# Transposing gathered rows on two row halves, ahead of the products, in a graph network's edge loop

## The chip, the cores and the metric

The kernel runs on one core of one Trainium2 chip. The metric is device time in microseconds (us) of one execution, as the median of several runs. The engines have these names in the profile: PE is TensorE (PEld its weight loads), DVE VectorE, ACT ScalarE, POOL GpSimd, SP SyncE.

## What is computed

One message-passing layer of a graph network on 6250 nodes with 128 features and 100000 edges, with a residual and a layer norm. All data are float32. The edges come sorted by destination.

```python
row, col = src, dst                                   # 100000 each
msg_in = concat([x[row], x[col]], axis=-1)            # 256 features
h = relu(msg_in @ Wm1 + bm1)                          # 256
h = relu(h @ Wm2 + bm2)                               # 256
messages = h @ Wm3 + bm3                              # 128
agg = segment_sum(messages, col) / clip(count(col), 1)
upd = relu(concat([x, agg]) @ Wn1 + bn1) @ Wn2 + bn2
out = layernorm(x + (x + upd))
```

## The kernel before

**Preparation.** `x[row] @ Wm1[:128]` equals a row of `A = x @ Wm1[:128]`, so the kernel computes A (`atab`) and B = x @ Wm1[128:] (`btab`, as three bfloat16 terms) once a node and keeps both in DRAM. It also turns the edge lists into columns: `srcT[:, g, j]` holds, for tile j of edge group g, the source row number of the edge that stands on each of the 128 partitions. `src_f` is the float copy of the list from which these columns are transposed (`columns`).

**The edge loop.** A group is 512 edges, four tiles of 128; there are 196 groups. The loop works on two groups at a time, 98 pairs, and is written out in Python as a pipeline of several stages with the order of TensorE, ScalarE, GpSimd, VectorE and SyncE written out by hand. One turn holds, on TensorE and in this order, work of four different pairs:

- `turned` (L594): six transposes of the partial sums of an older pair, which `add_up` (L603) on VectorE adds to the accumulator `acc`, eight windows of nodes.
- `first_layer` (L544, L549): the 128 x 256 tiles of gathered A rows are transposed into PSUM (`ph`, four banks: two groups i, two halves h of a group's columns), eight transposes of 128 x 128 a group; onto the same PSUM columns come the products of `bw` (rows of B for a narrow window of destinations, bfloat16) with `ohts`, a 0/1 matrix that spreads them over the edges, four a group. ScalarE adds the bias and applies relu (L556) and makes `h1`.
- `sums` (L575): a 0/1 matrix `oh` of 32 columns a tile adds up h2 over the edges of each node of a window. The four tiles of a group use four column groups of the array.
- `second_layer` (L565): h1 times `w2`, in four parts of two tiles each; VectorE applies bias and relu behind each part (L567) and makes `h2s[0]`, `h2s[1]`.

A float32 product of L565 or L575 stands in the profile as two matmul records, a transpose as one.

**The gathers.** `fetch` (L506) issues eight indirect DMAs a pair from GpSimd, one for each tile, with the row numbers in a column of `srcT`; they fill `rows`, which has two buffers. A pair's rows are thus fetched while the pair before it is still to be transposed: the first gather of a pair waits until the products of the pair two before it have read the buffer. Ahead of five of the eight gathers GpSimd copies one column (`seen`, L505) of something that ScalarE or VectorE has made; `made_by` says which:

```python
return {2: h1[:, 1, 1, 0:1], 3: h1[:, 0, 0, 0:1], 4: h2s[0][:, 0, 0:1], 5: h2s[0][:, 2, 0:1],
        7: h2s[1][:, 0, 0:1]}
```

That copy holds the queue of GpSimd until the named part of h1 or h2 is there. The SyncE queue brings the rows of B (L511), the ScalarE queue the edges' offsets `db` (L390).

After the loop, products over the nodes, the second half of the update, the layer norm and the stores make up the rest.

Of the kernel before, what the change touches and what calls it, by code (L numbers as in the profile page):

```python
# [9 lines left out]
F32 = mybir.dt.float32  # L10
BF16 = mybir.dt.bfloat16
I32 = mybir.dt.int32
# [7 lines left out]
P = 128  # L20
# [7 lines left out]
def kernel(  # L28
# [36 lines left out]
    nc = tc.nc  # L65
# [4 lines left out]
    GT = 4  # L70
    GE = GT * P
# [7 lines left out]
    NQ = 2 * WN  # L79
# [13 lines left out]
    srcT = const.tile([P, NG, GT], I32, name="srcT")  # L93
# [17 lines left out]
    ident = const.tile([P, P], F32, name="ident")  # L111
# [40 lines left out]
    with tc.tile_pool(name="prep", bufs=1) as prep, tc.tile_pool(  # L152
        name="brow", bufs=6
    ) as brow, tc.tile_pool(name="pp", bufs=3, space=PSUM) as pp, tc.tile_pool(
        name="pb", bufs=5, space=PSUM
# [4 lines left out]
        src_i = prep.tile([R, 2 * GE], I32, name="src_i", tag="src_i")  # L160
# [59 lines left out]
        nc.vector.tensor_reduce(most, real.rearrange("r s (j e) -> r (s j) e", j=GT), AX.X, ALU.max)  # L220

        src_f = prep.tile([R, 2, GT, P], F32, name="src_f", tag="dst_i")
        nc.vector.tensor_copy(src_f.rearrange("r s u e -> r (s u e)"), src_i)
        span_i = prep.tile([R, RT], I32, name="span_i")

        nc.vector.tensor_tensor(most, most, least, op=ALU.max)
# [217 lines left out]
        behind = list(X_BEHIND)  # L444
# [29 lines left out]
    with edge, tc.tile_pool(name="wk", bufs=2) as wk, tc.tile_pool(  # L474
        name="p1", bufs=1, space=PSUM
# [8 lines left out]
        h2s = [wk.tile([P, GT, H + 1], F32, name=f"h2_{i}", bufs=1) for i in range(NH2)]  # L484
# [6 lines left out]
        def flat_bank():  # L491
            return bank().rearrange("p t h -> p (t h)")

        seen = wk.tile([P, 1], F32, name="seen", bufs=1)

        def fetch(groups, queues, behind={}):


            rows = ld.tile([P, 2, (GT + 1) * H], F32, name="rows", bufs=2)
            got = []  # L500
            for i, ((idx, firsts), queue) in enumerate(zip(groups, queues)):
                ag = rows[:, i, :GT * H].rearrange("p (j h) -> p j h", j=GT)
                for j in range(GT):
                    if i * GT + j in behind:
                        nc.gpsimd.tensor_copy(seen, behind[i * GT + j])  # L505
                    nc.gpsimd.indirect_dma_start(  # L506
                        out=ag[:, j, :], out_offset=None, in_=atab[:, :],
                        in_offset=bass.IndirectOffsetOnAxis(ap=idx[:, j:j + 1], axis=0))
                bw = rows[:, i, GT * H:].bitcast(BF16).rearrange("p (k h) -> p k h", k=2)
                for h, first in enumerate(firsts):  # L510
                    queue.dma_start(bw[:, h, :], btab[ds(first, NW)].rearrange("n c h -> (n c) h")[:P])  # L511
                got.append((ag, bw))
            return got
# [21 lines left out]
            return oht, oh[:, :GT]  # L535


        def first_layer(got, ohts, nts):
            ph = p1.tile([P, 2, 2, HC, 2 * P], F32, name="ph")
            for i, ((ag, bw), nt) in enumerate(zip(got, nts)):  # L540
                for c in range(HC):
                    for j in range(nt):
                        h, k = divmod(j, 2)
                        nc.tensor.matmul(ph[:, i, h, c, k * P:(k + 1) * P], ag[:, j, c * P:(c + 1) * P], ident,  # L544
                                         is_transpose=True, start=(c == 0 and k == 0), stop=False,
                                         skip_group_check=True)
                for c in range(HC):
                    for h in range(nt // 2):
                        nc.tensor.matmul(ph[:, i, h, c, :], bw[:, h, c * P:(c + 1) * P],  # L549
                                         ohts[:, i, h * 2 * P:(h + 1) * 2 * P], start=False, stop=True,  # L550
                                         skip_group_check=True)
            h1 = wk.tile([P, 2, HC, GE], F32, name="h1")
            for i in reversed(range(len(nts))):
                nh = nts[i] // 2
                for c in range(HC):
                    nc.scalar.activation(h1[:, i, c, :nh * 2 * P].rearrange("p (h e) -> p h e", h=nh),  # L556
                                         ph[:, i, :nh, c, :], AF.Relu, bias=b1[:, c:c + 1])
            return h1

        def second_layer(h1, h2, nt):  # L560
            for j0 in range(0, nt, 2):
                ph2 = bank()
                for j in range(j0, j0 + 2):
                    for c in range(HC):
                        nc.tensor.matmul(ph2[:, j - j0, :], h1[:, c, j * P:(j + 1) * P],  # L565
                                         w2[:, c, :], start=(c == 0), stop=(c == HC - 1))
                nc.vector.tensor_tensor(h2[:, j0:j0 + 2, :H], ph2, nb2.to_broadcast([P, 2, H]), op=ALU.max)  # L567

        def sums(groups):

# [61 lines left out]
        NP = NG // 2  # L632
# [11 lines left out]
        def load_firsts(p):  # L644
            st[p]["firsts"] = [load_bases(tilei[0:1, g * GT:(g + 1) * GT], NTS[g], ENG.DVE) for g in (2 * p, 2 * p + 1)]

        def made_by(i):
            if i < 3:
                return {}
            h1 = st[i - 2]["h1"]  # L650
            return {2: h1[:, 1, 1, 0:1], 3: h1[:, 0, 0, 0:1], 4: h2s[0][:, 0, 0:1], 5: h2s[0][:, 2, 0:1],
                    7: h2s[1][:, 0, 0:1]}

        slots = list(range(SLOTS))

        def clear(n):
# [5 lines left out]
        for i in range(NP + 4):  # L662
            if i == 8:
                late_loads()

                none = wk.tile([16, (NG * GE - E) // 16 + 1], I32, name="none", bufs=1)
                nc.vector.memset(none, NONE)
                nc.sync.dma_start(dpad[E - 16:].rearrange("(p e) -> p e", p=16), none)
                nc.sync.dma_start(dpad[:E].rearrange("(p e) -> p e", p=16), dst.rearrange("(p e) -> p e", p=16))
            if i < NP:  # L670
                c = 2 * i // CG + 1
                if 2 * i % CG == 0 and 1 < c < NG // CG:
                    chunks[c] = chunk(c)
                queues = [(nc.sync, ENG.SP), (nc.scalar, ENG.Activation) if i == 0 else (nc.sync, ENG.SP)]
                firsts = [load_bases(pairi[0:1, g * 2:(g + 1) * 2], NTS[g] // 2, eng, NPAD - NW)
                          for g, (_, eng) in zip((2 * i, 2 * i + 1), queues)]
                got = fetch([(srcT[:, 2 * i + k, :], firsts[k]) for k in range(2)], [q for q, _ in queues],
                            made_by(i))
                st[i] = dict(nts=NTS[2 * i:2 * i + 2], got=got)
            p = i - 1  # L680
            if p < 0:
                continue
            if p == 0:
                make_hot(0)
            k = p - 3
            if k >= 0:
                if k < NP - 2:
                    load_firsts(k)
                firsts = st[k]["firsts"]
                pt = turned(st[k]["part"], st[k]["nts"])  # L690
                if k == NP - 1:
                    whole(rest)
                add_up(pt, firsts, st.pop(k)["nts"])
            for step, after in enumerate((10, 12, 13)):
                if i >= after and (i - after) % 4 == 0 and (i - after) // 4 < len(pieces):
                    double((i - after) // 4, step)
            if p + 1 < NP:
                make_hot(p + 1)
            if p == 0:
                clear(3)  # L700
            if p < NP:
                s = st[p]
                s["h1"] = first_layer(s.pop("got"), s.pop("ohts"), s["nts"])
            if p == 0:
                whole(x_part(X_FIRST, bank, (nc.scalar, nc.vector)))
            if 0 <= p - 2 < NP:
                st[p - 2]["part"] = part_of(summed(p - 2), st[p - 2]["nts"])
            if 0 <= p - 1 < NP:
                s = st[p - 1]
                for j, nt in enumerate(s["nts"]):  # L710
                    if p == NP and j == 1:
                        load_firsts(NP - 2)
                        load_firsts(NP - 1)
                    second_layer(s["h1"][:, j], h2s[j], nt)
            if p in (1, 2):
                clear(2)
        assert not st and not slots
# [6 lines left out]
        with tc.If(groups > 0):  # L724
            with tc.For_i(0, NG, 1) as g:
# [3 lines left out]
                with tc.For_i(0, more, 1):  # L729
                    for t, by in ((tilei[0:1, ds(g * GT, GT)], float(WB)), (pbase[:, ds(g, 1), :], float(WB)),  # L730
                                  (dloc[:, ds(g, 1), :], -float(WB))):
                        nc.vector.tensor_scalar(t, t, by, None, op0=ALU.add)
                    idx = wk.tile([P, GT], I32, name="idx")
                    nc.vector.tensor_copy(idx, srcT[:, ds(g, 1), :].rearrange("p o j -> p (o j)"))
                    pbc = wk.tile([P, 2], F32, name="pbc")
                    nc.vector.scalar_tensor_tensor(pbc, pbase[:, ds(g, 1), :].rearrange("p o k -> p (o k)"),
                                                   float(NPAD - NW), iota_p.to_broadcast([P, 2]),
                                                   op0=ALU.min, op1=ALU.add)
                    dl = wk.tile([P, GT], F32, name="dl")
                    nc.vector.tensor_copy(dl, dloc[:, ds(g, 1), :].rearrange("p o j -> p (o j)"))  # L740

                    ti = wk.tile([1, GT], I32, name="ti", bufs=1)
# [242 lines left out]
```

## Time and profile before

| | |
|---|---|
| median of three runs | 1281.67 us (1280.34 to 1282.84) |
| the profiled execution | 1284.33 us |
| its span, first to last instruction | 1282.5 us |
| granted TensorE clock, mean | 0.994 |
| TensorE busy | 1260.3 us, 98% |
| VectorE, ScalarE, GpSimd busy | 649.6, 379.3, 922.6 us |
| gathers (L506) | 784, 981 ns each |
| GpSimd copies (L505) | 475, 199 ns each |
| transposes of gathered rows (L544) | 1564 matmuls, 273 ns each as recorded |

Matmul records overlap, since TensorE is pipelined: the time that one takes of the engine is the step from its start to the next one's start, not its duration. A row of the timeline gives start, length, engine, line, operation, output <- inputs, rows x columns of the array in use, shape, count, and in brackets the idle time before it with what ended that. A row of a group gives total busy time, mean duration in ns, and idle time before the group's instructions.

### The profile page before, as it was taken

What the parts mean: (1) busy time and instruction counts of PE and PEld (TensorE: products, weight loads), DVE (VectorE), ACT (ScalarE), POOL (GpSimd) and SP (SyncE); (2) the same over time, 40 slices, a digit from 0 to 9 for tenths busy, and PEclk for the clock granted to TensorE, in tenths of its full rate; (3) what the DMA queues carried; (4) which work ended last, traced back from release to release, by engine and by line L of the source; (5) the groups of instructions that cost most, each with busy time, mean ns of one, the idle gap of its engine ahead of it and who ended that gap; (6) DMA issues with size and microseconds to landing.
All of it is one profiled execution on the core that took longest, in us unless ns stands there. A gap on an engine that the chain in (4) does not pass through costs nothing. (4 is left out here: it accounts for less than half of the span.)

```text
span 1282.5 us, 25680 instructions
## 1 busy us (share of the span) xinstructions
PE 1260.3 (98%) x8291; PEld 1046.3 (82%) x8292; DVE 649.6 (51%) x1684; ACT 379.3 (30%) x768; POOL 922.6 (72%) x1341
## 2 busy tenths in 40 slices
PE   7999999999999999999999999999999999999998
PEld 5758888888888888888888888888888888888666
DVE  6774444444445444444444444444444444444677
ACT  4652222222222222222222222222222222222156
POOL 5658887777777777777778777777777777785032
PEclk9899999999999999999999999999999999999999
DMA  5976555555555555545555545544455544453153
GB/s 176 356 251 174 153 149 155 143 161 157 140 148 158 151 151 156 150 138 157 159 146 151 143 144 140 144 141 132 139 142 141 144 136 134 138 145 98 34 159 103
DMA packets 147517, 193.52 MB, mean 151 GB/s; under 512 B 23248, under 2 KB 100578, under 8 KB 147364
## 3 DMA queue, kind: packets, MB, share of 16 engines
q0 software_dynamic: 38160, 103.75, 29.9%
q1 hardware_dynamic: 94528, 62.02, 15.6%
q10 hardware_dynamic: 14692, 26.09, 6.8%
q8 instruction: 66, 1.08, 0.3%
q14 instruction: 71, 0.58, 0.1%
HBM read 169.06 MB, written 23.08 MB: 150 GB/s over the span
## 5 line engine op out<-in xcount | busy, mean ns | idle before, releaser
L506 POOL DMA_INDIRECT rows<-atab,srcT x784 | 769.2, 981 | 246.9 <-issue 114.5
L565 PE MATMUL bank<-w,h 128*128 128x256 f32 x3128 | 701.4, 382 | 0.1
L565 PEld LDWEIGHTS bank<-w,h 128*128 128x128 f32 x3128 | 586.1, 190 | 116.3 <-PE bank L575 39.7
L567 DVE TENSOR_TENSOR h<-bank,nb 128x512 f32<-128x512 f32 x391 | 270.8, 693 | 521.1 <-PE bank L565 506.9
L556 ACT ACTIVATE h<-ph,b 128x512 f32<-128x512 f32 x392 | 236.8, 687 | 820.2 <-PE ph L549 820.2
L603 DVE TENSOR_TENSOR acc<-acc,bank 128x63 f32 x782 | 172.6, 221 | 67.5 <-DVE h L567 34.2
L544 PE MATMUL ph<-ident,rows 128*128 128x128 f32 x1564 | 203.8, 273 | 1.4 <-ACT h L556 0.8
L544 PEld LDWEIGHTS ph<-ident,rows 128*128 128x128 f32 x1564 | 177.6, 142 | 3.7 <-ACT h L556 1.7
L549 PE MATMUL ph<-oht,rows 128*128 128x256 bf16 x782 | 118.2, 274 | 1.7 <-DMA rows<-btab 1.7
L575 PE MATMUL bank<-h,oh 128*32 128x257 f32 x1564 | 105.5, 386 | 0.6 <-DVE acc L603 0.6
L505 POOL COPY seen<-h 128x1 f32<-128x1 f32 x475 | 94.7, 199 | 2.0
L549 PEld LDWEIGHTS <-rows 128*128 128x128 bf16 x782 | 76.7, 98 | 8.8 <-DMA rows<-btab 2.0
L594 PE MATMUL bank<-ident,part 128*128 128x128 f32 x588 | 80.3, 272 | 0.0
L594 PEld LDWEIGHTS bank<-ident,part 128*128 128x128 f32 x588 | 69.9, 140 | 10.4 <-issue 0.4
L575 PEld LDWEIGHTS bank<-h,oh 128*32 128x32 f32 x1564 | 40.8, 109 | 38.4 <-DVE acc L603 19.4
L583 ACT COPY part<-bank 128x257 f32<-128x257 f32 x196 | 65.3, 402 | 14.0 <-PE bank L575 14.0
L808 POOL TENSOR_TENSOR agg<-total,rc 128x512 f32<-128x512 f32 (+2 forms) x15 | 16.0, 1070 | 74.3 <-DVE total L805 36.0
L273 PE MATMUL pbt<-w,xT 128*128 128x256 f32 x196 | 47.6, 390 | 10.3 <-DVE rest L298 10.0
L273 PEld LDWEIGHTS pbt<-w,xT 128*128 128x128 f32 x196 | 37.1, 196 | 17.2 <-DVE rest L298 10.7
L518 DVE TENSOR_SCALAR oht<-db,iota_p 128x1024 bf16<-128x1024 bf16 x98 | 47.6, 486 | 0.0
L520 DVE TENSOR_TENSOR oh<-iota_n,dloc 128x256 f32<-128x256 f32 x98 | 40.9, 417 | 0.0
L845 PEld LDWEIGHTS pot<-wu,u 128*128 128x128 f32 x192 | 23.6, 192 | 4.8 <-issue 4.3
(139 smaller groups left out, 446.5 us busy)
## 6 DMA issues: line engine op xcount, KB each, us to landing
db<-reltab ACTq DMA_DIRECT2D x98, 256.0 KB, 4.2
rows<-btab SPq DMA_DIRECT2D x389, 64.0 KB, 3.4
rows<-atab,srcT POOLq DMA_INDIRECT x784
btab<-acc SPq DMA_DIRECT2D x24, 384.0 KB, 5.0
atab<-at SPq DMA_DIRECT2D x24, 256.0 KB, 5.4
xd<-in_x_dram SPq DMA_DIRECT2D x12, 256.0 KB
x2tab<-xd SPq DMA_DIRECT2D x12, 256.0 KB
x_sb<-in_x_dram SPq DMA_DIRECT2D x5, 512.0 KB
```

Of the source, the lines that this page charges most:

```text
L273: nc.tensor.matmul(pbt[:, a, :], xT[:, (t0 + a) * P:(t0 + a + 1) * P], w1[:, k, :], start=True, stop=True)
L505: nc.gpsimd.tensor_copy(seen, behind[i * GT + j])
L506: nc.gpsimd.indirect_dma_start(out=ag[:, j, :], out_offset=None, in_=atab[:, :], in_offset=bass.IndirectOffsetOnAxis(ap=idx[:, j:j + 1], a ...
L544: nc.tensor.matmul(ph[:, i, h, c, k * P:(k + 1) * P], ag[:, j, c * P:(c + 1) * P], ident, is_transpose=True, start=(c == 0 and k == 0), st ...
L549: nc.tensor.matmul(ph[:, i, h, c, :], bw[:, h, c * P:(c + 1) * P], ohts[:, i, h * 2 * P:(h + 1) * 2 * P], start=False, stop=True, skip_gro ...
L556: nc.scalar.activation(h1[:, i, c, :nh * 2 * P].rearrange("p (h e) -> p h e", h=nh), ph[:, i, :nh, c, :], AF.Relu, bias=b1[:, c:c + 1])
L565: nc.tensor.matmul(ph2[:, j - j0, :], h1[:, c, j * P:(j + 1) * P], w2[:, c, :], start=(c == 0), stop=(c == HC - 1))
L567: nc.vector.tensor_tensor(h2[:, j0:j0 + 2, :H], ph2, nb2.to_broadcast([P, 2, H]), op=ALU.max)
L575: nc.tensor.matmul(pg[j * WN:(j + 1) * WN, :H + 1], oh[:, j, :], h2[:, j, :], start=True, stop=True, skip_group_check=True)
L583: nc.scalar.copy(part[:nt * WN, i], pg[:nt * WN, :H + 1])
L594: nc.tensor.matmul(pt[:, c, :n], rows, ident[:n, :n], is_transpose=True, start=True, stop=True, skip_group_check=True)
L603: nc.vector.tensor_add(window, window, pts[i][:, :, j * WN:j * WN + WB])
```

## The change

1. *Row halves.* Each 128 x 128 transpose becomes two of 64 rows: rows 0 to 63 and rows 64 to 127 of a gathered tile, each against a 64 x 64 piece of the identity. The halves alternate, and go to different PSUM banks (half h of the rows to bank h of the group). For this the edges are dealt out anew over tiles and partitions: partition 64 h + e of tile u holds edge 256 h + 64 u + e of its group, where it was edge 128 j + p on partition p of tile j. `src_f` is written in that order, by two copies instead of one. The order of edges in h1 stays as it was.
2. *Order.* The transposes of both groups of a pair run first, then the products of both; before, each group's transposes and products followed each other.
3. *Gathers.* The copies on GpSimd and `made_by` are gone. The last four gathers of a pair (those of its second group) take their row numbers from small tiles (`idx_0`, `idx_1`, `idx_2`) that VectorE copies out of `srcT` (`hold`), behind the first and second part of `h2s[0]` and the first part of `h2s[1]`, a turn ahead. The other four read `srcT` and wait for nothing but the buffer.

In the rarely taken path behind the loop three small tiles get one buffer instead of two. The diff, cut to its core:

```diff
-        nc.vector.tensor_copy(src_f.rearrange("r s u e -> r (s u e)"), src_i)
+        for s in range(2):
+            nc.vector.tensor_copy(src_f[:, s].rearrange("r u (h e) -> r u h e", h=2),
+                                  src_i[:, s * GE:(s + 1) * GE].rearrange("r (h u e) -> r u h e", h=2, u=GT))
...
-        seen = wk.tile([P, 1], F32, name="seen", bufs=1)
+        held = {}
+        def hold(i, cols):
+            if i < NP:
+                t = wk.tile([P, len(cols)], I32, name=f"idx_{cols[0]}")
+                nc.vector.tensor_copy(t, srcT[:, 2 * i + 1, cols[0]:cols[-1] + 1])
+                held.setdefault(i, {}).update({c: t[:, k:k + 1] for k, c in enumerate(cols)})
 
-        def fetch(groups, queues, behind={}):
+        def fetch(groups, queues, last={}):
...
                 for j in range(GT):
-                    if i * GT + j in behind:
-                        nc.gpsimd.tensor_copy(seen, behind[i * GT + j])
+                    at = last.get(j, idx[:, j:j + 1]) if i else idx[:, j:j + 1]
                     nc.gpsimd.indirect_dma_start(
                         out=ag[:, j, :], out_offset=None, in_=atab[:, :],
-                        in_offset=bass.IndirectOffsetOnAxis(ap=idx[:, j:j + 1], axis=0))
+                        in_offset=bass.IndirectOffsetOnAxis(ap=at, axis=0))
...
+        halves = [slice(h * NQ, (h + 1) * NQ) for h in range(2)]      # NQ = 64
...
                 for c in range(HC):
-                    for j in range(nt):
-                        h, k = divmod(j, 2)
-                        nc.tensor.matmul(ph[:, i, h, c, k * P:(k + 1) * P], ag[:, j, c * P:(c + 1) * P], ident,
-                                         is_transpose=True, start=(c == 0 and k == 0), stop=False,
-                                         skip_group_check=True)
+                    for u in range(GT):
+                        for h in range(nt // 2):
+                            nc.tensor.matmul(ph[:, i, h, c, u * NQ:(u + 1) * NQ], ag[halves[h], u, c * P:(c + 1) * P],
+                                             ident[halves[h], halves[h]], is_transpose=True,
+                                             start=(c == 0 and u == 0), stop=False, skip_group_check=True)
+            for i, ((ag, bw), nt) in enumerate(zip(got, nts)):
                 for c in range(HC):
                     for h in range(nt // 2):
                         nc.tensor.matmul(ph[:, i, h, c, :], bw[:, h, c * P:(c + 1) * P],
...
-        def second_layer(h1, h2, nt):
+        def second_layer(h1, h2, nt, holds=()):
...
                 nc.vector.tensor_tensor(h2[:, j0:j0 + 2, :H], ph2, nb2.to_broadcast([P, 2, H]), op=ALU.max)
+                if j0 // 2 < len(holds):
+                    hold(*holds[j0 // 2])
...
-                            made_by(i))
+                            held.pop(i, {}))
...
-                    second_layer(s["h1"][:, j], h2s[j], nt)
+                    second_layer(s["h1"][:, j], h2s[j], nt,
+                                 (((p + 2, (2, 3)),) if j else ((p + 2, (0,)), (p + 2, (1,)))))
```

More of the change, by code (lines that the diff above doesn't have):

```diff
@@ L645, in load_firsts @@
             st[p]["firsts"] = [load_bases(tilei[0:1, g * GT:(g + 1) * GT], NTS[g], ENG.DVE) for g in (2 * p, 2 * p + 1)]
[L647 to L652, printed above, removed]
         slots = list(range(SLOTS))
@@ L732 @@
                         nc.vector.tensor_scalar(t, t, by, None, op0=ALU.add)
-                    idx = wk.tile([P, GT], I32, name="idx")
+                    idx = wk.tile([P, GT], I32, name="idx", bufs=1)
                     nc.vector.tensor_copy(idx, srcT[:, ds(g, 1), :].rearrange("p o j -> p (o j)"))
-                    pbc = wk.tile([P, 2], F32, name="pbc")
+                    pbc = wk.tile([P, 2], F32, name="pbc", bufs=1)
                     nc.vector.scalar_tensor_tensor(pbc, pbase[:, ds(g, 1), :].rearrange("p o k -> p (o k)"),
@@ L738 @@
                                                    op0=ALU.min, op1=ALU.add)
-                    dl = wk.tile([P, GT], F32, name="dl")
+                    dl = wk.tile([P, GT], F32, name="dl", bufs=1)
                     nc.vector.tensor_copy(dl, dloc[:, ds(g, 1), :].rearrange("p o j -> p (o j)"))
```

## The prediction

> **What bounds the kernel now.** I read the page's head first, then the busy time by window inside the edge loop, then the timeline of TensorE over one turn of that loop.
>
> ```profile
> span 1282.5 us, 25680 instructions
> PE 1260.3 (98%) x8291; PEld 1046.3 (82%) x8292; DVE 649.6 (51%) x1684; ACT 379.3 (30%) x768; POOL 922.6 (72%) x1341
> ```
>
> ```profile
> 400.00:700.00 300.00, 300.00 (x2061) 254.17 (x2061) 143.07 (x379) 76.91 (x156) 233.03 (x342) 1.00 0.54 150
> ```
>
> The second fence is a stretch of 300 us in mid-loop: TensorE (first pair of numbers) is busy for all 300.00, at a granted clock of 1.00; VectorE for 143, GpSimd for 233. So a turn is as long as TensorE's work in it, and what shortens or lengthens that work is what counts. Its timeline:
>
> ```profile
> 606.02 0.82 PE L594 MATMUL bank<-ident,part 128*128 128x128 f32 x6
> 606.67 1.04 PE L544 MATMUL ph<-ident,rows 128*128 128x128 f32 x8
> 607.55 0.60 PE L549 MATMUL ph<-oht,rows 128*128 128x256 bf16 x4
> 607.99 1.04 PE L544 MATMUL ph<-ident,rows 128*128 128x128 f32 x8
> 608.86 0.60 PE L549 MATMUL ph<-oht,rows 128*128 128x256 bf16 x4
> 609.39 1.07 PE L575 MATMUL bank<-h,oh 128*32 128x257 f32 x16
> 610.39 7.17 PE L565 MATMUL bank<-w,h 128*128 128x256 f32 x32
> 617.40 0.82 PE L594 MATMUL bank<-ident,part 128*128 128x128 f32 x6
> 618.06 0.38 PE L544 MATMUL ph<-ident,rows 128*128 128x128 f32 x2
> ```
>
> Matmuls overlap, so I go by starts, not by durations. One turn (two groups of 512 edges) is 618.06 - 606.67 = 11.39 us. The 16 transposes of L544 take 607.55 - 606.67 = 0.88 and 608.86 - 607.99 = 0.87, together **1.75 us, 109 ns each**. That is the part which the change rewrites. The four products behind them take 0.44 us, 0.11 each.
>
> Two more readings decide what a transpose costs. First, what sets its 109 ns: in the preparation the same kind of transpose runs with 98 moving columns.
>
> ```profile
> 52.83 0.25 PE L352 MATMUL pd<-ident,dst_f 98*128 98x98 f32 x1
> ...
> 53.42 0.25 PE L353 MATMUL ps<-ident,src_f 98*128 98x98 f32 x1
> ```
>
> Seven steps lie between these two of eight, so one step is 0.59/7 = 84 ns; 109 x 98/128 is 83. The time goes by the moving columns, and the weight load of 128 columns, which these have too, hides within 84 ns.
>
> Second, half-height transposes stand in the trace once, at the end of the loop, where the last group fills only 64 partitions:
>
> ```profile
> 1207.55 0.26 PEld L594 LDWEIGHTS bank<-ident,part 64*128 64x128 f32 x3 [0.23 <-ACT part L583]
> 1207.88 0.19 PEld L366 LDWEIGHTS bank<-xT,wu 128*128 128x128 f32 x1
> ```
>
> ```profile
> L594 PEld LDWEIGHTS bank<-ident,part 64*128 64x128 f32 x3 | 0.3, 136 | 0.2 <-ACT part L583 0.2
> L594 PE MATMUL bank<-ident,part 64*128 64x64 f32 x3 | 0.4, 238 | 0.0
> ```
>
> Three loads span 0.26 us and one lasts 0.136, so they start (0.26 - 0.136)/2 = **62 ns** apart. By columns, 64 would take 109/2 = 55 ns; the load keeps it a little above that. All three sit in the same row half, so this is the price of one half alone.
>
> **TensorE, part by part.** A turn now holds 32 half transposes (64 rows, 64 moving columns) where it held 16, ordered low half, high half, low half, high half, each half writing its own PSUM bank. If two halves run side by side, a pair takes 62 ns and 16 pairs take 0.99 us; if they follow one another, a pair takes 124 and they take 1.98. No row shows two row halves at once. The nearest is the sums, L575, which use four column groups of 32: 16 matmuls of 257 columns start over 610.39 - 609.39 = 1.00 us, where one after another they would need 16 x 257 x 109/128 ns = 3.5 us. So groups of the array do work side by side here, and their loads too:
>
> ```profile
> 609.39 0.59 PEld L575 LDWEIGHTS bank<-h,oh 128*32 128x32 f32 x16 [0.21 <-DVE acc L603]
> L575 PEld LDWEIGHTS bank<-h,oh 128*32 128x32 f32 x1564 | 40.8, 109 | 38.4 <-DVE acc L603 19.4
> ```
>
> Sixteen loads of 109 ns each lie in 0.59 us. I take 62 ns a pair, with 54.5 (columns alone) and 124 as its ends.
>
> The Trainium skill, page "TensorEngine Tiling (Array Packing)", section "Key Properties", says that different tiles can execute LdWeights and Matmul in parallel; by that page too the pair would take the time of one half. No run here shows it for row halves yet.
>
> The other cost is the change of the array's shape. The last three-transpose batch starts its third at about 1207.55 + 0.12 + 0.06 = 1207.73 and streams for 55 ns, to 1207.78; the next full-height load starts at 1207.88, 0.10 later. In the loop, the last product starts at 608.86 + 3 x 0.11 = 609.19, streams to 609.30, and the first load of the sums starts at 609.39, 0.09 later. So a change of shape drains for about 95 ns, and the next load lies open behind it. The change adds two of them a turn: into row halves in front of the first transpose (95 + a load of about 55 = 0.15 us) and out of them in front of the products (95 + a bf16 load). The latter's open part is small: bf16 loads last 98 ns where the transposes' last 142, so about 55 - 44 = 11 ns, 0.11 us in all. Running both groups' transposes ahead of both groups' products is what keeps it at two and not four. I take 0.26 us, ends 0.20 and 0.35.
>
> ```profile
> L544 PEld LDWEIGHTS ph<-ident,rows 128*128 128x128 f32 x1564 | 177.6, 142 | 3.7 <-ACT h L556 1.7
> L549 PEld LDWEIGHTS <-rows 128*128 128x128 bf16 x782 | 76.7, 98 | 8.8 <-DMA rows<-btab 2.0
> ```
>
> Sum: 0.99 + 0.26 = 1.25 us instead of 1.75, **0.50 us less a turn**. There are 1564/16 = 97.75 turns' worth: 49 us. A pair breaks even at (1.75 - 0.26)/16 = 93 ns.
>
> **What is late next: VectorE's additions.** Between the second layer and the sums VectorE adds up windows for 2.07 us, which does not shrink, and the row of L575 above puts 19.4 us of waiting down to that. If the sums really waited for it, nothing would be gained. They do not:
>
> ```profile
> 607.27 2.07 DVE L603 TENSOR_TENSOR acc<-acc,bank 128x63 f32 x8 [0.36 <-DVE h L567]
> ...
> 620.62 0.22 DVE L603 TENSOR_TENSOR acc<-acc,bank 128x63 f32 x1 [0.15 <-DVE acc L603]
> ```
>
> ```profile
> 620.77 0.86 PE L575 MATMUL bank<-h,oh 128*32 128x257 f32 x12
> ```
>
> In the turn shown, the additions end at 609.34 and the sums start at 609.39, which looks like a wait. One turn later the eighth addition ends at 620.84, and the sums had started at 620.77. The 0.21 us is the drain. What needs the additions is a PSUM bank of the second layer behind the sums, over 1 us further on, so 0.5 us fits.
>
> **GpSimd.** Removed: 475 copies, about five a turn. The time of eight gathers:
>
> ```profile
> 609.73 1.17 POOL L506 DMA_INDIRECT rows<-atab,srcT  x1 [1.12 <-PE ph L549]
> 611.21 0.95 POOL L506 DMA_INDIRECT rows<-atab,srcT  x1 [0.30 <-ACT h L556]
> 612.16 0.20 POOL L505 COPY seen<-h 128x1 f32<-128x1 f32 x1
> 612.51 0.97 POOL L506 DMA_INDIRECT rows<-atab,srcT  x1 [0.15 <-issue]
> ...
> 616.48 0.97 POOL L506 DMA_INDIRECT rows<-atab,srcT  x1 [0.16 <-issue]
> 617.75 0.94 POOL L506 DMA_INDIRECT rows<-atab,srcT  x1 [0.30 <-issue]
> ...
> 621.12 1.15 POOL L506 DMA_INDIRECT rows<-atab,srcT  x1 [1.10 <-PE ph L549]
> ```
>
> With a copy between them gathers start 1.30 apart (612.51 - 611.21), without one 1.27 (617.75 - 616.48): a copy mostly fills a gap that is there anyway. Back to back, eight gathers need 1.48 + 7 x 1.27 = 10.37 us; the turn would be 10.89. GpSimd then idles 0.5 us instead of the 1.1 seen here, and taking the copies away is worth nothing on the path (with them it would be about 10.6, still under). The landing of the last gather has nearly a whole turn in hand, since its rows are read one turn after the next.
>
> **VectorE's new copies.** Three small copies a turn; the nearest row of that size is 149 ns:
>
> ```profile
> L175 DVE COPY x_sb<-xT 128x1 f32<-128x1 f32 x4 | 0.6, 149 | 1.7 <-ACT xT L321 1.7
> ```
>
> ```profile
> 612.49 0.69 DVE L567 TENSOR_TENSOR h<-bank,nb 128x512 f32<-128x512 f32 x1 [2.42 <-PE bank L565]
> 614.22 0.69 DVE L567 TENSOR_TENSOR h<-bank,nb 128x512 f32<-128x512 f32 x1 [1.03 <-PE bank L565]
> 615.95 0.69 DVE L567 TENSOR_TENSOR h<-bank,nb 128x512 f32<-128x512 f32 x1 [1.04 <-PE bank L565]
> ```
>
> Each follows one of h2's parts, behind which VectorE idles about 1.0 us, so they are hidden. Each waits for the gather that last read its buffer, two turns back, whose rows TensorE has already transposed by then. The gathers behind them: the fifth starts at about 609.73 + 1.48 + 3 x 1.27 = 615.0 and needs the part that ends at 613.18; the sixth at 616.3 needs the one that ends at 614.91; the seventh at 617.6 the one that ends at 616.64. All are 0.9 us or more early, so no gather waits. If that cover went, GpSimd has 0.5 us a turn. In the preparation one conversion of src becomes two of half the size with a permuted pattern: under 0.2 us, once, beside TensorE's work.
>
> **The sum.** The profiled execution took 1284.33 us, 2.7 above the median of the three timed runs (1281.67). 1284.33 - 49 = 1235.3; from the median, 1232.7. I forecast **1233**. About 0.2%, 2.6 us, is what a measurement of this kernel can tell from no change.
>
> **Rivals.**
> - *The loads of the two halves go one behind the other.* The half-height load was not shorter for its fewer rows (136 ns against 142), so 32 loads may simply cost twice 16. A pair then takes at least 2 x 54.5 = 109 and at most 124 ns: 1.74 to 1.98 + 0.26 is 0.25 to 0.49 us more a turn, 24 to 48 us: **1306 to 1330, slower**. It decides from 93 ns a pair on. For it: no row with two row halves at work. Against: the column groups' loads overlap. The Trainium skill, page "TensorE: Matmul & The Clock Gate", section "LDWEIGHTS (loading the stationary operand)", has this rule (time by columns, whatever the rows) with 128/1.2 = 107 ns a load, which single-file would be an estimate of 3.4 us a turn; the trace agrees on the rows and not on the figure, its loads being 62 ns apart. Chance 0.16.
> - *Halves overlap in part*, a pair at 70 to 95 ns (small instructions that cannot be issued as fast, or PSUM writes that meet): 1.12 to 1.52 + 0.26 gives 0.37 less to nothing: **1246 to 1284**. Chance 0.09.
> - *VectorE or GpSimd takes over.* A turn is held by the additions, or by gathers that wait for the copied row numbers, at about its present length: **1277 to 1290**. Against: the margins above. Chance 0.03.
>
> My case has 0.72, with its own range 1215 (pairs at 54.5, changes of shape 0.20: 1.07 us, 0.68 less, 66 us) to 1246. The range reaches on into the second rival: **1215 to 1272**. Faster: 0.72 + 0.07 = 0.79; within 0.2%: 0.03; slower: 0.18.
>
> **What would show it.** In the timeline of a turn, from the first half transpose to the first product 1.1 to 1.2 us; a turn of 10.9; low and high half starting nearly together; a gap of about 0.1 us on either side of the transposes; GpSimd idle about 0.5 us a turn in front of the first gather, none behind h2. Pairs 93 ns apart or more, a turn of 11.4 or more, or TensorE idle in the loop would prove me wrong.

## The result and the profile after

The changed kernel takes 1234.28 us (median of four runs, 1232.48 to 1235.16), the kernel before 1281.76 in the same comparison (1280.34 to 1282.84): a ratio of 0.9627, 95% interval 0.9614 to 0.9639. The forecast was 1233, with 1215 to 1272 around it. The profiled execution took 1235.1 us. The head of its page, and the same 300 us of mid-loop as before:

```profile
span 1233.3 us, 28237 instructions
PE 1212.0 (98%) x9855; PEld 975.8 (79%) x9856; DVE 668.1 (54%) x1970; ACT 380.0 (31%) x768; POOL 803.2 (65%) x866
```

```profile
400.00:700.00 300.00, 300.00 (x2579) 245.41 (x2572) 154.80 (x474) 82.81 (x168) 210.02 (x221) 1.00 0.56 158
```

TensorE is still busy for all 300.00 us, at the full granted clock. It is still the bound, and it does more turns in the same time. One turn on its timeline (L554 are now the half transposes, L560 the products, L588 the sums, L576 the second layer, L607 the partial sums' transposes):

```profile
606.53 1.07 PE L588 MATMUL bank<-h,oh 128*32 128x257 f32 x16
607.53 7.17 PE L576 MATMUL bank<-w,h 128*128 128x256 f32 x32
614.54 0.82 PE L607 MATMUL bank<-ident,part 128*128 128x128 f32 x6
615.29 1.21 PE L554 MATMUL ph<-ident,rows 64*128 64x64 f32 x32
616.44 1.05 PE L560 MATMUL ph<-oht,rows 128*128 128x256 bf16 x8
617.41 1.07 PE L588 MATMUL bank<-h,oh 128*32 128x257 f32 x16
```

The turn is 617.41 - 606.53 = 10.88 us, 0.51 less by these rounded starts. Taken over all 98 groups of sums, the median step is 11.383 us before and 10.887 after: 0.496 less, and 97.75 x 0.496 = 48.5 us, against 47.5 between the two medians. From the first half transpose to the first product is 616.44 - 615.29 = 1.15 us. The other stretches keep their lengths, but for the gap of 615.29 - 614.54 - 6 x 0.109 = 0.10 us ahead of the transposes, which is new: the array changes its shape there. How the halves run shows in a window of 0.1 us, 615.20 to 615.30, that holds the start of the stretch:

```profile
615.29 0.14 PEld L554 LDWEIGHTS ph<-ident,rows 64*128 64x128 f32 x2 [0.17 <-issue]
```

Two loads, of 134 ns or more each, lie in 0.14 us: the low and the high half load together. The rest of the stretch follows that beat: 1.15 us less one drain (the gap at a change of shape) and one half's stream at its end (0.095 + 0.055) and the first load (0.055) is 0.945 us for 15 steps of a pair, 63 ns each. The trace's single records agree: from the start of the second pair (615.403) to that of the sixteenth (616.279) are 14 steps of 62.6 ns, and the two halves of a pair start 3 or 4 ns apart.

### The profile page after: what moved, and what is told of

Read it like the earlier page. It is cut to its first block, busy times and chain, and to the rows that moved or that the text cites. A ratio compares the mean times of both kernels' runs of the same rounds, so it can differ in the third digit from the quotient of the medians.

```text
span 1233.3 us, 28237 instructions
## 1 busy us (share of the span) xinstructions
PE 1212.0 (98%) x9855; PEld 975.8 (79%) x9856; DVE 668.1 (54%) x1970; ACT 380.0 (31%) x768; POOL 803.2 (65%) x866
## 5 line engine op out<-in xcount | busy, mean ns | idle before, releaser
L576 PE MATMUL bank<-w,h 128*128 128x256 f32 x3128 | 701.4, 382 | 0.1
L576 PEld LDWEIGHTS bank<-w,h 128*128 128x128 f32 x3128 | 586.1, 190 | 116.3 <-PE bank L588 39.7
L514 POOL DMA_INDIRECT rows<-atab,srcT x404 | 384.4, 952 | 201.0 <-PE ph L560 99.9
L514 POOL DMA_INDIRECT rows<-atab,idx x380 | 359.8, 947 | 116.8 <-issue 106.2
L554 PE MATMUL ph<-ident,rows 64*128 64x64 f32 x3128 | 119.3, 226 | 2.0 <-ACT h L567 0.8
L554 PEld LDWEIGHTS ph<-ident,rows 64*128 64x128 f32 x3128 | 105.6, 139 | 19.8 <-issue 16.6
L588 PE MATMUL bank<-h,oh 128*32 128x257 f32 x1564 | 105.5, 386 | 0.5 <-DVE acc L616 0.5
L560 PE MATMUL ph<-oht,rows 128*128 128x256 bf16 x782 | 102.6, 274 | 0.3 <-DMA rows<-btab 0.3
L607 PE MATMUL bank<-ident,part 128*128 128x128 f32 x588 | 80.3, 272 | 0.0
L560 PEld LDWEIGHTS <-rows 128*128 128x128 bf16 x782 | 68.5, 98 | 13.8 <-DMA rows<-btab 0.5
L607 PEld LDWEIGHTS bank<-ident,part 128*128 128x128 f32 x588 | 69.9, 139 | 10.4 <-issue 0.4
L588 PEld LDWEIGHTS bank<-h,oh 128*32 128x32 f32 x1564 | 40.8, 109 | 38.4 <-DVE acc L616 18.7
L502 DVE COPY idx<-srcT 128x1 int32<-128x1 int32 (+1 forms) x285 | 42.7, 150 | 0.0
```

The source lines that it names most:

```text
L514: nc.gpsimd.indirect_dma_start(out=ag[:, j, :], out_offset=None, in_=atab[:, :], in_offset=bass.IndirectOffsetOnAxis(ap=at, axis=0))
L554: nc.tensor.matmul(ph[:, i, h, c, u * NQ:(u + 1) * NQ], ag[halves[h], u, c * P:(c + 1) * P], ident[halves[h], halves[h]], is_transpose=Tru ...
L588: nc.tensor.matmul(pg[j * WN:(j + 1) * WN, :H + 1], oh[:, j, :], h2[:, j, :], start=True, stop=True, skip_group_check=True)
L607: nc.tensor.matmul(pt[:, c, :n], rows, ident[:n, :n], is_transpose=True, start=True, stop=True, skip_group_check=True)
```

## The experiments

All are compared with the kernel before in runs on the same chip. Their medians there were 1281.68 to 1282.32.

**1. The halves one after another.** All low halves of a pair of groups first, then all high halves:

```diff
-            for i, ((ag, bw), nt) in enumerate(zip(got, nts)):
-                for c in range(HC):
-                    for u in range(GT):
-                        for h in range(nt // 2):
+            for h in range(2):
+                for i, ((ag, bw), nt) in enumerate(zip(got, nts)):
+                    for c in range(HC):
+                        for u in range(GT if h < nt // 2 else 0):
```

> The changed kernel with all transposes of the low row half first, then all of the high half, the same 32 instructions a turn. Theory (a pair costs what one half costs because neighbours in program order sit on different row halves): nearly 31 steps of 62 ns instead of 16, 0.94 us more a turn, 92 us, 1326 us. Rival (half transposes are just cheaper, or the engine looks far enough ahead to pair them itself): 1234 us, within 3.

Measured: 1311.54 us, ratio 1.023 (1.0215 to 1.0246), slower than the kernel before. The direction and the cause hold, the size was 15 us too high. TensorE's timeline of this kernel, and the matmuls of the transposes in two stretches of 0.40 us (busy time and count of PE, then of PEld):

```profile
606.84 0.82 PE L607 MATMUL bank<-ident,part 128*128 128x128 f32 x6
607.59 2.01 PE L554 MATMUL ph<-ident,rows 64*128 64x64 f32 x32
609.54 1.05 PE L560 MATMUL ph<-oht,rows 128*128 128x256 bf16 x8
...
619.28 2.02 PE L554 MATMUL ph<-ident,rows 64*128 64x64 f32 x32
```

```profile
608.35:608.75 0.40, 0.40 (x13) 0.40 (x12) 1.00 0.63 174
609.00:609.40 0.40, 0.40 (x10) 0.40 (x8) 1.00 0.00 0
```

The stretch to the first product is 1.95 us where it was 1.15, and the turn 619.28 - 607.59 = 11.69. Less the same 0.205 at its ends, 1.745 us is 28 steps of 62 ns. The 32 starts would be 31 steps with no overlap at all, and 30 by the expectation, which had put one overlap at the seam; there are three. At the seam, where the last low halves and the first high halves stand side by side in the program, three more matmuls touch 0.40 us of time (13) than later on (10). So the engine does run two halves together where they are near each other in its order, here over three steps, and not the halves that stand further apart. The count of instructions and the work in them are those of the changed kernel; the alternation of the halves alone is worth 1311.5 - 1234.3 = 77 us, and without it the row halves lose 30 us against full transposes. This is the rival of the prediction, made real: had the loads gone one behind the other, the change would have been slower.

**2. The price of a change of shape.** Each group's products put back behind its own transposes:

```diff
                                              start=(c == 0 and u == 0), stop=False, skip_group_check=True)
-            for i, ((ag, bw), nt) in enumerate(zip(got, nts)):
                 for c in range(HC):
                     for h in range(nt // 2):
```

> The changed kernel with the products of each group put back right behind that group's transposes: four changes of the array's shape around the transposes in a turn instead of two. Theory (each change of shape drains about 95 ns and lays the next load open; in and out of row halves 0.15 + 0.11 us): 0.26 us more a turn, 25 us, 1234 + 25 = 1259 us. Rival (the order is worth nothing, or what it gives is earlier rows, not drains): 1234 us, within 3.

Measured: 1258.02 us, ratio 0.9812 (0.9797 to 0.9827), and a turn of 11.147 us as the median over all turns: 0.260 more than in the changed kernel. TensorE's timeline (here L559 are the products, L587 the sums):

```profile
605.43 0.72 PE L554 MATMUL ph<-ident,rows 64*128 64x64 f32 x16
606.08 0.61 PE L559 MATMUL ph<-oht,rows 128*128 128x256 bf16 x4
606.62 0.72 PE L554 MATMUL ph<-ident,rows 64*128 64x64 f32 x16
607.27 0.61 PE L559 MATMUL ph<-oht,rows 128*128 128x256 bf16 x4
607.82 1.07 PE L587 MATMUL bank<-h,oh 128*32 128x257 f32 x16
```

Four products stream for 0.44 us, but the next start of a transpose is 606.62 - 606.08 = 0.54 away: 0.10 of drain. The load behind it and the drain on the other side are in the stretch of the transposes: 606.08 - 605.43 = 0.65 us, where eight pairs at 62 ns are 0.50. Two more changes of shape cost what the prediction put on two.

**3. The order without the halves.** The kernel before with both groups' full transposes ahead of both groups' products, and nothing else:

```diff
                                          skip_group_check=True)
+            for i, ((ag, bw), nt) in enumerate(zip(got, nts)):
                 for c in range(HC):
```

> The kernel before with the order alone changed: full transposes of both groups of a pair first, then the products of both. Theory (without row halves there is no change of shape between transposes and products, so the order saves none): 1281.8 us, within 2. Rival (the order gives something by itself): 1279 us or less.

Measured: 1281.71 us, ratio 0.9996 (0.9987 to 1.0005). Without row halves there is no drain between transposes and products that this order could save.

**4. The gathers' part alone, and the rest without it.** The first kernel below is the one before with GpSimd's copies replaced by the row numbers that VectorE copies; the second is the changed kernel with the copies back and nothing held; in the third both are gone.

```diff
# the kernel before, gathers' part alone
-                    if i * GT + j in behind:
-                        nc.gpsimd.tensor_copy(seen, behind[i * GT + j])
+                    at = last.get(j, idx[:, j:j + 1]) if i else idx[:, j:j + 1]
...
# the changed kernel, copies back
-                    at = last.get(j, idx[:, j:j + 1]) if i else idx[:, j:j + 1]
+                    if i * GT + j in behind:
+                        nc.gpsimd.tensor_copy(seen, behind[i * GT + j])
...
# the changed kernel, neither
-            if i < NP:
+            if False:
                 t = wk.tile([P, len(cols)], I32, name=f"idx_{cols[0]}")
```

> The kernel before with the gathers' part of the change alone: no copies on GpSimd, the last four gathers of a pair read row numbers copied by VectorE; full transposes and the old order. Theory (GpSimd is idle 1.1 us a turn, off the path): 1281.8 us, within 2. Rival (GpSimd's copies held the turn): a good part of the 47 us, 1270 us or less.

Measured: 1281.59 us, ratio 0.9999 (0.9989 to 1.0008).

> The changed kernel with the copies on GpSimd of the kernel before in place of the held row numbers; row halves and order as changed. Theory (eight gathers with five copies need about 10.3 to 10.6 us back to back, under the turn of 10.89): 1234 us, within 2. Rival (a turn this short is held by GpSimd once the copies are back): 1240 us or more, and TensorE idle in front of the transposes.

Measured: 1234.66 us, ratio 0.9632 (0.9619 to 0.9645).

> The changed kernel without the held row numbers and without copies on GpSimd: all eight gathers read the row numbers where they stand and wait for nothing but the buffer and their queue. Theory (the parts of h2 are ready before the gathers that wait for them, so the wait holds nothing): 1234 us, within 2. Rival (the wait spreads the gathers' traffic, and without it they collide with the rows of B or the offsets): 1240 us or more, with TensorE waiting for DMA.

Measured: 1234.00 us, ratio 0.9624 (0.961 to 0.9637).

The turn's median is 11.383 us in the first, as before, and 10.887 in the other two, as after, to the nanosecond. So this part of the change moves nothing here, with full or half transposes, and neither does holding gathers back at all. GpSimd's timeline says why. The changed kernel:

```profile
606.87 0.94 POOL L514 DMA_INDIRECT rows<-atab,srcT  x1 [1.04 <-PE ph L560]
608.12 0.95 POOL L514 DMA_INDIRECT rows<-atab,srcT  x1 [0.30 <-issue]
...
611.87 0.95 POOL L514 DMA_INDIRECT rows<-atab,idx  x1 [0.30 <-issue]
...
615.62 0.95 POOL L514 DMA_INDIRECT rows<-atab,idx  x1 [0.30 <-issue]
617.76 0.94 POOL L514 DMA_INDIRECT rows<-atab,srcT  x1 [1.19 <-PE ph L560]
```

With the copies back (there L508 and L507):

```profile
607.35 0.95 POOL L508 DMA_INDIRECT rows<-atab,srcT  x1 [0.83 <-PE ph L554]
...
609.89 0.97 POOL L508 DMA_INDIRECT rows<-atab,srcT  x1 [0.16 <-issue]
610.87 0.19 POOL L507 COPY seen<-h 128x1 f32<-128x1 f32 x1
611.22 0.97 POOL L508 DMA_INDIRECT rows<-atab,srcT  x1 [0.15 <-issue]
...
616.42 0.96 POOL L508 DMA_INDIRECT rows<-atab,srcT  x1 [0.15 <-issue]
618.23 0.95 POOL L508 DMA_INDIRECT rows<-atab,srcT  x1 [0.85 <-PE ph L554]
```

Both end a turn waiting for the products to free the buffer, 1.19 and 0.85 us. The gathers of this turn do not wait for the held numbers: the idle time before one that reads `idx` is the same 0.30 as before the others, and over all 380 of them it is 116.8 us, 0.31 each. The copies on VectorE lie where they were expected, in the gaps behind h2's parts:

```profile
609.56 0.69 DVE L578 TENSOR_TENSOR h<-bank,nb 128x512 f32<-128x512 f32 x1 [1.85 <-PE bank L576]
610.17 0.15 DVE L502 COPY idx<-srcT 128x1 int32<-128x1 int32 x1
611.29 0.69 DVE L578 TENSOR_TENSOR h<-bank,nb 128x512 f32<-128x512 f32 x1 [0.97 <-PE bank L576]
```

**5. What the prices point to.** If a pair of halves costs 62 ns instead of 109, and a change of shape about 0.1 us and an open load, two more steps follow. First, the six transposes of the partial sums, which stand right ahead of the half transposes, go on row halves too, with a PSUM bank for each half:

```diff
-            pts = []
+            pts = [flat_bank()[:, :2 * (HC + 1) * NQ].rearrange("p (i c q) -> p i c q", i=2, q=NQ) for _ in halves]
             for i, nt in enumerate(nts):
-                n = nt * WN
-                pt = flat_bank()[:, :(HC + 1) * P].rearrange("p (c q) -> p c q", q=P)
                 for c in range(HC + 1):
...
+                    for h in range(nt // 2):
...
+                        nc.tensor.matmul(pts[h][:, i, c, :], rows, ident[halves[h], halves[h]], is_transpose=True,
+                                         start=True, stop=True, skip_group_check=True)
...
-                    nc.vector.tensor_add(window, window, pts[i][:, :, j * WN:j * WN + WB])
+                    k = j % 2 * WN
+                    nc.vector.tensor_add(window, window, pts[j // 2][:, i, :, k:k + WB])
```

> The changed kernel with the six transposes of the older pair's partial sums on row halves too, low and high half in a PSUM bank each (twelve half transposes ahead of the 32, no further change of shape). Theory (a pair of halves costs 62 ns where a full transpose costs 109): 6 x (109 - 62) = 0.28 us less a turn, 27 us, 1207 us. Rival (VectorE's additions, which then need both banks' halves, or the gathers become the bound at a turn of 10.6): 1220 to 1234 us with TensorE idle in the loop.

Measured: 1208.42 us, ratio 0.9428 (0.9414 to 0.9443); a turn of 10.597 us. Second, `first_layer` is cut in two and the sums run between the transposes and the products:

```diff
+                ph = transposed(s["got"], s["nts"])
+            if 0 <= p - 2 < NP:
+                pgs = summed(p - 2)
+            if p < NP:
-                s["h1"] = first_layer(s.pop("got"), s.pop("ohts"), s["nts"])
+                s["h1"] = first_layer(ph, s.pop("got"), s.pop("ohts"), s["nts"])
...
-                st[p - 2]["part"] = part_of(summed(p - 2), st[p - 2]["nts"])
+                st[p - 2]["part"] = part_of(pgs, st[p - 2]["nts"])
```

> The changed kernel with the sums moved in between the half transposes and the products: the array goes from row halves to column groups of 32 to its full shape, three changes of shape a turn instead of four, and the second layer follows the products in the same shape. Theory (each change drains about 95 ns and lays the next load open; the one in front of the second layer, 0.20 us, goes): 0.20 us less a turn, 19 us, 1215 us. Rival (changing between two split shapes costs as much more, or ScalarE's h1, 0.9 us later, or the sums' inputs are late): 1230 us or more.

Measured: 1215.84 us, ratio 0.9481 (0.9466 to 0.9495); a turn of 10.693 us.

> Both: the partial sums' transposes on row halves and the sums in between. Theory: 0.48 us less a turn, 10.41 us, 46 us, 1188 us. Rival (GpSimd, which needs 10.0 us for eight gathers back to back, or VectorE takes over): 1195 us or more, with TensorE idle in the loop.

Measured: **1188.58 us**, ratio 0.9267 (0.9253 to 0.9281), faster than both kernels. Its TensorE (L610 partial sums' transposes, L554 half transposes, L591 sums, L563 products, L579 second layer), and its 300 us of mid-loop:

```profile
602.72 0.58 PE L610 MATMUL bank<-ident,part 64*128 64x64 f32 x12
603.14 1.17 PE L554 MATMUL ph<-ident,rows 64*128 64x64 f32 x32
604.23 1.07 PE L591 MATMUL bank<-h,oh 128*32 128x257 f32 x16
605.24 1.05 PE L563 MATMUL ph<-oht,rows 128*128 128x256 bf16 x8
606.12 7.07 PE L579 MATMUL bank<-w,h 128*128 128x256 f32 x32
613.13 0.58 PE L610 MATMUL bank<-ident,part 64*128 64x64 f32 x12
```

```profile
400.00:700.00 300.00, 300.00 (x2894) 246.82 (x2893) 166.75 (x500) 84.22 (x172) 220.44 (x231) 1.00 0.58 164
```

A turn is 613.13 - 602.72 = 10.41 us. From the first product to the second layer is 606.12 - 605.24 = 0.88, eight times 0.11, with no drain; in the changed kernel the second layer followed the sums after 607.53 - 606.53 = 1.00 us, of which the column groups' work (four rounds of 257 columns at 109/128 ns) is 0.875. TensorE is still never idle. GpSimd now comes close:

```profile
606.56 0.96 POOL L514 DMA_INDIRECT rows<-atab,srcT  x1 [0.72 <-PE ph L563]
607.83 0.94 POOL L514 DMA_INDIRECT rows<-atab,srcT  x1 [0.30 <-issue]
...
616.96 1.21 POOL L514 DMA_INDIRECT rows<-atab,srcT  x1 [0.70 <-PE ph L563]
```

It has 0.4 us a turn left above its constant 0.30, so in a version shorter still the copies on GpSimd might begin to count: in experiment 4 gathers with a copy between them start 1.29 to 1.33 us apart (611.22 - 609.89), without one 1.25 in the changed kernel. That was not tried.

## Why the prediction was right

- *A pair of halves costs what one half costs, 62 ns.* Right: 63 ns from the stretch of 1.15 us. It was taken from three half transposes in one row half at the end of the loop before, and from column groups that load and stream together. Experiment 1 shows that the side-by-side running is the cause: 77 us hang on it. The Trainium skill's statement on the page "TensorEngine Tiling (Array Packing)", section "Key Properties", that different tiles can load and multiply in parallel, holds here for two row halves: the two loads lie in 0.14 us. The rule of the Trainium skill's page "TensorE: Matmul & The Clock Gate", section "LDWEIGHTS (loading the stationary operand)", that rows do not matter, holds too (139 ns recorded for a half, 142 for a full one), but it does not make the change a loss, since the two halves' loads share the time.
- *Two changes of shape cost 0.26 us.* Right: 0.260 by experiment 2.
- *0.50 us a turn, 49 us.* Right: 0.496 us, 48.5; by the medians 47.5.
- *The additions are not waited for.* Right: the row of the sums' loads still puts 18.7 us down to them in the changed kernel, where it was 19.4, while the turn lost its 0.5 us in full. In the changed kernel's turn above the sums start at 617.41, and the additions end only at 615.79 + 2.07 = 617.86:

```profile
615.79 2.07 DVE L616 TENSOR_TENSOR acc<-acc,bank 128x63 f32 x8 [0.36 <-DVE h L578]
```

- *GpSimd's copies and VectorE's are worth nothing.* Right by experiment 4, in both directions. The size of GpSimd's slack was wrong: I gave it 0.5 us and a first step of 1.48 between gathers; it had 1.19 in the turn shown, 0.89 of it above the constant 0.30, since all seven steps between the eight gathers are 1.25. What made the first gather of a turn longer before (1.17 us against 0.94) was not settled.
- *One expectation behind it missed its size*: halves apart were put at 1326 us and took 1311.5, because the engine overlaps a few instructions at the seam, which I had counted as one step and which were three: two steps of 62 ns a turn are 12 of the 14.5 us.

## What to carry to other kernels

A float32 transpose on TensorE costs by its moving columns here, 109 ns for 128 and 84 for 98; one with 64 takes 62 ns alone, a little above that. Two half-height transposes that stand next to each other in program order, on different row halves and in different PSUM banks, do the same work in 62 ns; the same two far apart in the order cost 125. No run put both halves into one bank, so whether the banks have to differ is not shown. Each change of the array's shape has a price, here 0.1 us of drain and the next weight load in the open, so work of one shape belongs together, and a stage that can move to where its shape fits is worth moving. Waits and copies on an engine that idles for the bound one every turn can be left out of the reckoning, after a look at how much idle time is left.

## What the runs showed of the hardware that was not expected

The side-by-side running does not need exact alternation: blocks of sixteen halves still overlapped by three steps of 62 ns at their seam. And a change between two split shapes, from row halves straight to column groups of 32, costs no more than one to or from the full array: experiment 5 moved the sums into that place and the turn fell by 10.887 - 10.693 = 0.194 us, against 0.20 expected for the change of shape that went.
